# Last layer and output projection with the features in rows, in an attention block with a gated feed-forward network

## Chip, cores and metric

The kernel runs on one core of a Trainium2 chip. The metric is the device time of one execution in microseconds, the median of several runs; a profile of one further execution is shown beside it. The engines are named as the profile names them: PE (TensorE, matmuls; PEld are its weight loads), DVE (VectorE), ACT (ScalarE), POOL (GpSimd) and SP (the engine whose queue issues nearly all DMAs here).

## What is computed

The input is x of 8 sequences, each of 512 tokens with 256 features. Cut to what matters:

```python
xn = layernorm(x)                                   # over the 256 features
q, k, v = heads(xn @ in_proj_w.T)                   # 16 heads of 16; q and k are then rotated
p = softmax(where(0 <= t - s < 250, q @ k.T / 4, -inf))
s_ = merge(p @ v) @ out_proj_w.T                    # attention, 256 features
h = 2 * relu(s0 * concat(xn, -xn) @ sign(k0))       # 1024 features
h = 2 * relu(s1 * h @ sign(k1))                     # 1024
z = s2 * h @ sign(k2)                               # 256: the last layer
out = x + s_ * silu(z)
```

sign(k) is 1 where the boolean k holds and -1 elsewhere.

## The kernel before

Everything is written out without loops on the chip, one sequence b after another; B = 8, T = 512, P = 128. Within a sequence x is normalized with the tokens in the partitions (norm), turned on PE so that the features lie in the partitions (turn_x), and projected to v, k and q (project_v, project). The rotated q and k go to DRAM and come back in groups of four heads (to_dram, stack; on SP). Attention runs in nine steps: scores (sc, in two PSUM tiles), exponentials on ACT, masks on POOL (affine_select), and one step later the product with v (po). po has one PSUM bank; after a group of heads, keep (L690) empties it to V and S, on ACT for even groups and on DVE for odd ones. S holds the sums of the softmax; divisions inverts it in four pieces (L754), and divide shuffles it to R and multiplies V by R on POOL (L763), with a comparison on POOL (L767) and a count on DVE (L772) behind.

The feed-forward layers are exact in two parts: each activation is held as an f16 high part and an fp32r low part, so that h1, h2 and z take one set of matmuls for each (layer, L415; last, L441). Of a finished block of h, ACT writes the high part (L426) and then DVE the low part (L424); after the second the PSUM bank is free. ps_m has three such banks, tag "mm", shared by turn_x, v, q, k, h1, h2, z and the projection.

last makes z for 128 tokens at a time: the tokens are the stationary side, so z has the tokens in its partitions and 256 features in its columns. DVE scales it to gate (L467). gate_ready makes silu from it: an exponential on ACT (L496), the addition of 1 on POOL (L499), a reciprocal on DVE (L503) and a product on POOL (L504). project_o does the output projection for the same 128 tokens (att_ps, L782), fetches the same rows of x once more (xr, L787), multiplies by the gate on DVE (L804), adds xr on POOL (L809) and stores (L810). In the last sequence h2 is made in two halves of 256 tokens; z 0 and 1 are "soon", z 2 and 3 "final": their exponential comes straight from PSUM (L450), the reciprocal is L459, and the last output takes its own way (L794 to L798).

The order on each engine is the program's order, and a planner writes it. Each piece has a key, in units of which a sequence has SEQ = 42, and a cost; run sorts the pieces by key and sends follow-ups (pairs of a delay and a function) when the clock of summed costs has passed them. The layers of sequence b+1 begin at SEQ * (b + 1), and the z of sequence b stand between its h1 blocks:

```python
return SEQ * (b + 1) + 2 * L1 * (t + 1) + L3 * t            # last_at, b + 1 < B
return SEQ * (b + 1) + (32.0 + 3.2 * t if b + 2 < B else 18.0 + 2.5 * t)   # late
```

last_at is the key of z, late that of the projection, and gate_ready comes 4 units ahead of it. The pieces of attention are then placed among the keys of the layers (quick).

Of the kernel before, what the change touches and what calls it, by code (L numbers as in the profile page):

```python
# [11 lines left out]
F32 = mybir.dt.float32  # L12
# [4 lines left out]
ALU = mybir.AluOpType  # L17
# [17 lines left out]
def tile_attention_times_gated_ffn(  # L35
    ctx: ExitStack,
    tc: tile.TileContext,
    x: bass.AP,
    w_qkv: bass.AP,
    w_o: bass.AP,  # L40
    k0: bass.AP,
# [1 line left out]
    k2: bass.AP,  # L43
    s: bass.AP,
    rope: bass.AP,
    out: bass.AP,
):

# [22 lines left out]
    nc = tc.nc  # L73
    P = 128
    B, T, E = x.shape
    H = HEADS
    D = E // H
    NT = T // P
    EC = E // P
    F0, F1 = k0.shape[1], k1.shape[1]  # L80
    NF0, NF1 = F0 // P, F1 // P
# [10 lines left out]
    turned = ctx.enter_context(tc.tile_pool(name="turned", bufs=1))  # L92
    work = ctx.enter_context(tc.tile_pool(name="work", bufs=2))
# [105 lines left out]
    SEQ = 42.0  # L199
    L1, L2, L3 = 0.87, 3.45, 1.87  # L200
    states = {}
# [224 lines left out]
        high = lambda: nc.scalar.activation(hi, ph, AF.Relu)  # L426
        return [(0.0, high), (0.6 if f + 1 < NF0 else 0.0, low)]

    def last(b, t, how):
        st = states[b]  # L430
        pz = ps_m.tile([P, E], F32, tag="mm", name=f"z_ps_{b}_{t}")
        if how == "at once":
            for c in range(NF1):
                nc.tensor.matmul(
                    pz, st["h2p"][:, c, ts(t, P)], w2["l"][:, c].bitcast(F32),
                    start=(c == 0), stop=(c == NF1 - 1),
                )
        else:
            for p in "hl":
                for c in range(NF1):  # L440
                    nc.tensor.matmul(  # L441
                        pz, st["h2" + p][:, c, ts(t, P)], w2[p][:, c],
                        start=(c == 0 and p == "h"), stop=(c == NF1 - 1 and p == "l"),
                    )
        gate = st["gate", t] = outs.tile([P, E], F32, tag=f"gate{t}", name=f"gate_{b}_{t}")
        if how == "final":
            den = denominator(b, t)

            def ends():
                nc.scalar.activation(den, pz, AF.Exp, scale=scales[:, 1:2])  # L450
                nc.vector.tensor_scalar(gate, pz, scales[:, 0:1], None, ALU.mult)
                return [(0.3, add)]

            def add():
                nc.scalar.activation(den, den, AF.Identity, bias=1.0)
                return [(0.3, invert_)]

            def invert_():
                nc.vector.reciprocal(den, den)  # L459
                if t + 1 < NT:  # L460
                    nc.gpsimd.tensor_tensor(gate, gate, den, ALU.mult)
                st["den"] = den

            return [(0.0, ends)]

        def scale():
            nc.vector.tensor_scalar(gate, pz, scales[:, 0:1], None, ALU.mult)  # L467
            if how != "later":
                return [(0.5 if t == 0 else 4.5, lambda: gate_ready(b, t))]

        return [(0.0, scale)]

# [14 lines left out]
                    )  # L487
                nc.scalar.activation(h[:, f], ps, AF.Relu)

    def denominator(b, t):  # L490
        return work.tile([P, E], F32, tag="den", name=f"den_{b}_{t}")

    def gate_ready(b, t):
        st = states[b]
        gate, den = st["gate", t], denominator(b, t)
        nc.scalar.activation(den, gate, AF.Exp, scale=-1.0)  # L496

        def add():
            nc.gpsimd.tensor_scalar(den, den, 1.0, None, ALU.add)  # L499
            return [(0.9, invert_)]  # L500

        def invert_():
            nc.vector.reciprocal(den, den)  # L503
            return [(1.8, lambda: nc.gpsimd.tensor_tensor(gate, gate, den, ALU.mult))]  # L504

        return [(0.5, add)]

# [1 line left out]

    HALF = NF1 * L2 / 2 + 2 * L3  # L510

    def last_at(b, t):

        if b + 1 < B:
            return SEQ * (b + 1) + 2 * L1 * (t + 1) + L3 * t
        half = t // 2
        return SEQ * b + NF0 * L1 + NT * L3 + HALF * (half + 1) - 2 * L3 + L3 * (t % 2)

    def late(b, t):

        if b + 1 == B and t >= NT // 2:
            return last_at(b, NT - 1) + L3 + 0.9 * (t - NT // 2)
        if b + 1 == B:
            return SEQ * b + 40.0 + 0.9 * t
        return SEQ * (b + 1) + (32.0 + 3.2 * t if b + 2 < B else 18.0 + 2.5 * t)

    def finish_ffn(b, t, how):
        quick.add(last_at(b, t))
        out = [(last_at(b, t), L3, lambda: last(b, t, how))]
        if how == "later":  # L530
            out.append((late(b, t) - 4.0, 0, lambda: gate_ready(b, t)))
        return out

    def ffn(b):

        now = SEQ * b + (NT * L3 if b == 0 else 0)
        out = []
        for f in range(NF0):
            quick.add(now)
            out.append((now, L1, lambda f=f: layer(b, "h1", "x", w0, f)))  # L540
            now += L1
            if f % 2 and b > 0:
                now += L3
        if b + 1 == B:
            for half in range(2):
                cols = ts(half, T // 2)
                for f in range(NF1):
                    quick.add(now)
                    out.append((
                        now, L2 / 2,  # L550
                        lambda f=f, cols=cols: layer(b, "h2", "h1", w1, f, cols=cols),
                    ))
                    now += L2 / 2
                now += 2 * L3
            return out
        for f in range(NF1):
            quick.add(now)
            for i in range(2):
                out.append(
                    (now, L2 / 2, lambda f=f, i=i: layer(b, "h2", "h1", w1, f, i, 2))  # L560
                )
                now += L2 / 2
        return out
# [211 lines left out]

        return [(2.0, product)]

    def project_o(b, t, final=False):
        st = states[b]
        pp = ps_m.tile([P, E], F32, tag="mm", name=f"att_ps_{b}_{t}")  # L780
        for c in range(EC):
            nc.tensor.matmul(  # L782
                pp, st["V", c][:, ts(t, P)], wo_sb[:, c, :],
                start=(c == 0), stop=(c == EC - 1),
            )
        xr = work.tile([P, E], F32, tag="xr", name=f"xr_{b}_{t}")
        nc.sync.dma_start(xr, x[b, ts(t, P), :])  # L787
        st["xr", t] = xr
        if final and t + 1 == NT:
            att = work.tile([P, E], F32, tag="xn", name=f"att_{b}_{t}")  # L790

            def out_of_psum():
                y, den = st["gate", t], st["den"]
                nc.scalar.copy(att, pp)  # L794
                nc.gpsimd.tensor_tensor(y, y, att, ALU.mult)
                nc.vector.tensor_tensor(y, y, den, ALU.mult)
                nc.vector.tensor_tensor(y, y, xr, ALU.add)
                nc.sync.dma_start(out[b, ts(t, P), :], y)  # L798

            return [(0.0, out_of_psum)]  # L800

        def product():
            y = st["gate", t]
            nc.vector.tensor_tensor(y, pp, y, ALU.mult)  # L804
            return [(1.0 if final else 0.5, store)]

        def store():
            y = st.pop(("gate", t))
            nc.gpsimd.tensor_tensor(y, y, xr, ALU.add)  # L809
            nc.sync.dma_start(out[b, ts(t, P), :], y)  # L810

        return [(0.0, product)]

    def finish(b, final=False):
        out = []
        for t in range(NT):
            end = final and t >= NT // 2
            out.append((late(b, t), 0.87, lambda t=t, end=end: project_o(b, t, end)))
        return out

    def divisions(b):
# [42 lines left out]
        everything.append((at, 0, lambda f=f, w=w, e=engine: make_w1(f, w, e)))  # L864
    for b in range(B):
        everything += prepare(b) + ffn(b)
        for t in range(NT):
            how = "later" if b + 1 < B else "soon" if t < NT // 2 else "final"
            everything += finish_ffn(b, t, how)
            if b + 1 < B:  # L870
                at = SEQ * b + 1.5 if b else 2.0
                everything.append((at + t, 0, lambda b=b, t=t: load_x(b + 1, t)))
        everything += divisions(b) + finish(b, b + 1 == B)
# [55 lines left out]
    with tc.If(found < n_rows):  # L929
        for b in range(B):  # L930
            for t in range(NT):
                load_x(b, t)
            run(prepare(b, plain=True))
            plain_ffn(b)
            for t in range(NT):
                run(finish_ffn(b, t, "at once"))
            for g in range(NG):
                stack(b, g)
                po = ps_o.tile([P, T], F32, tag="po", name=f"f_po_{b}_{g}")
                for t in range(NT):  # L940
                    for r in range(4):
                        shifted(b, g, t, r, po)
                keep(b, g, po)
            run(divisions(b))
            run(finish(b))
# [58 lines left out]
```

## Time and profile before

| | us |
|---|---|
| median of 3 runs | 627.94 (627.25 to 629.54) |
| the profiled execution, its own time | 628.36 |
| its span in the profile | 626.6 |
| from one kb_ps to the next, sequences 1 to 6 | 75.0 |

| engine | busy us | idle us before its work, largest cause |
|---|---|---|
| PE | 608.6 | 2.8, the identity matrix at the start |
| DVE | 394.1 | 48.5, h2l for ACT's h2h |
| ACT | 299.7 | 140.2, h2h for PE's h_ps |
| POOL | 316.2 | 104.0, masks for ACT's p |

Busy time counts an instruction from its start to its end. Matmuls overlap in the profile, so that what one costs is read from the distance between starts. A line of a group gives the line of the kernel, the engine, the operation, the tile written and the tile read, partitions by elements, and how many there were. The granted clock was 0.996 of full speed over the span.

### The profile page before, as it was taken

The numbers are of one execution on the slowest core, as the hardware profiler recorded it, in microseconds if no ns is written. First come the engines' busy times: TensorE is split into PE (matmuls) and PEld (weight loads), VectorE is DVE, ScalarE is ACT, GpSimd is POOL, SyncE is SP. The second block draws the span as 40 slices with busy tenths as digits, with TensorE's granted clock in tenths as the row PEclk, the third lists the DMA queues.
The fourth block names the chain that finished last, engine by engine and source line by source line (L and its number), as shares of the span: only waits on it lengthen the run. The fifth ranks groups of instructions, "written<-read, shape, count | busy, mean of one in ns | idle before, by whom it ended". The sixth has DMA issues, their size and how long they took to land.

```text
span 626.6 us, 12051 instructions
## 1 busy us (share of the span) xinstructions
PE 608.6 (97%) x4842; PEld 398.4 (64%) x4842; DVE 394.1 (63%) x667; ACT 299.7 (48%) x441; POOL 316.2 (50%) x409
## 2 busy tenths in 40 slices
PE   8899999999999999999999999999999999999994
PEld 6455576556665567655676566765676556767793
DVE  6773535667575774766658576485665668456573
ACT  4566655534554445545354454453444544564411
POOL 2954542456533655427634366235662356638641
PEclk9999999999999999999999999999999999999998
DMA  9352721116311263114421252412532116230101
GB/s 273 117 197 95 260 85 51 51 68 216 122 51 51 87 208 110 52 51 172 139 93 51 75 214 76 143 33 86 208 94 88 51 69 227 77 109 19 53 18 48
DMA packets 38193, 67.20 MB, mean 107 GB/s; under 512 B 5104, under 2 KB 19184, under 8 KB 38128
## 3 DMA queue, kind: packets, MB, share of 16 engines
q1 hardware_dynamic: 36384, 64.24, 30.5%
q10 hardware_dynamic: 1744, 2.10, 1.0%
q8 instruction: 40, 0.66, 0.4%
q14 instruction: 25, 0.20, 0.1%
HBM read 36.96 MB, written 29.36 MB: 106 GB/s over the span
## 4 chain that ended last, share of the span: by engine, by line
PE 85%; DVE 5%; POOL 3%; DMA 3%; ACT 2%; issue 1%; SPq 0%; POOLq 0%; ACTq 0%; DVEq 0%
PE h_ps L415 41%; PE po L679 11%; PE z_ps L441 9%; PE sc L605 8%; PE v_ps L292 4%; PE att_ps L782 4%; PE qa_ps L307 2%; PE kb_ps L307 2%; PE qb_ps L307 2%; DMA kb<-in_k_dram 2%; PE ka_ps L307 2%; PE xnT_ps L268 1%; DVE den L503 1%; DVE h2l L424 1%; DVE xn L250 1%
## 5 line engine op out<-in xcount | busy, mean ns | idle before, releaser
L624 ACT ACTIVATE p<-sc 128x1024 f32<-128x1024 f32 (+2 forms) x144 | 138.5, 1013 | 75.0 <-PE sc L605 41.0
L415 PE MATMUL h_ps<-h1l,w1l_sb 128*128 128x512 f32 (+1 forms) x576 | 144.2, 392 | 0.0
L640 POOL TENSOR_SCALAR_AFFINE_SELECT p<-p 128x512 f32<-128x512 f32 x128 | 90.3, 711 | 104.0 <-ACT p L624 104.0
L415 PE MATMUL h_ps<-h1h,w1h_sb 128*128 128x512 f16 (+1 forms) x576 | 123.0, 356 | 0.5 <-ACT v_pad L299 0.5
L415 PEld LDWEIGHTS h_ps<-h1l,w1l_sb 128*128 128x128 f32 x576 | 99.5, 188 | 25.7 <-issue 6.8
L426 ACT ACTIVATE h2h<-h_ps 128x512 f16<-128x512 f32 (+1 forms) x72 | 39.6, 550 | 140.3 <-PE h_ps L415 140.2
L415 PEld LDWEIGHTS <-w1h_sb 128*128 128x128 f16 x576 | 51.5, 98 | 55.1 <-issue 13.4
L679 PE MATMUL po<-p,v_pad 128*32 128x378 f32 (+4 forms) x1216 | 77.2, 372 | 1.3 <-DVE S L703 1.1
L647 POOL TENSOR_SCALAR_AFFINE_SELECT p<-p 128x512 f32<-128x512 f32 (+1 forms) x96 | 50.0, 521 | 54.6 <-ACT p L624 49.7
L424 DVE SCALAR_TENSOR_TENSOR h2l<-h_ps,h2h 128x512 fp32r<-128x512 f32 (+1 forms) x72 | 44.3, 617 | 48.5 <-ACT h2h L426 48.5
L503 DVE RECIPROCAL den<-den 128x256 f32<-128x256 f32 x30 | 52.5, 1752 | 28.2 <-POOL den L499 28.1
L424 DVE SCALAR_TENSOR_TENSOR h1l<-h_ps,h1h 128x512 fp32r<-128x512 f32 x64 | 42.4, 675 | 34.8 <-ACT h1h L426 34.8
L605 PEld LDWEIGHTS sc<-q,k 32*128 32x128 f32 x1216 | 44.1, 184 | 26.1 <-issue 15.0
L754 DVE RECIPROCAL S<-S 128x128 f32<-128x128 f32 x64 | 58.9, 933 | 0.0
L426 ACT ACTIVATE h1h<-h_ps 128x512 f16<-128x512 f32 x64 | 38.2, 597 | 41.8 <-PE h_ps L415 41.2
L605 PE MATMUL sc<-q,k 32*128 32x378 f32 (+4 forms) x1216 | 57.2, 306 | 0.0
L415 PE MATMUL h_ps<-xl,w0l_sb 128*128 128x512 f32 x128 | 52.5, 491 | 0.0
L679 PEld LDWEIGHTS po<-p,v_pad 128*32 128x32 f32 x1216 | 31.3, 109 | 30.8 <-issue 16.2
L809 POOL TENSOR_TENSOR gate<-gate,xr 128x256 f32<-128x256 f32 x31 | 25.1, 810 | 46.8 <-DMA xr<-in_x_dram 41.2
L441 PE MATMUL z_ps<-w2l_sb,h2l 128*128 128x256 f32 x256 | 38.3, 291 | 0.4 <-DVE h2l L424 0.4
L415 PE MATMUL h_ps<-xh,w0h_sb 128*128 128x512 f16 x128 | 38.6, 383 | 0.0
L339 POOL TENSOR_TENSOR m_ka<-m_ka,m_kb 128x512 f32<-128x512 f32 x16 | 20.1, 1278 | 30.3 <-DVE m_kb L319 30.3
(97 smaller groups left out, 811.0 us busy)
## 6 DMA issues: line engine op xcount, KB each, us to landing
q<-dq SPq DMA_DIRECT2D x64, 256.0 KB, 3.6
dq<-qh SPq DMA_DIRECT2D x16, 512.0 KB, 3.4
dq<-m_qa SPq DMA_DIRECT2D x16, 512.0 KB, 5.0
k<-dk SPq DMA_DIRECT2D x32, 256.0 KB, 2.8
dk<-kh SPq DMA_DIRECT2D x8, 512.0 KB, 2.6
dk<-m_ka SPq DMA_DIRECT2D x8, 512.0 KB, 2.6
xr<-in_x_dram SPq DMA_DIRECT2D x32, 128.0 KB, 2.8
out_dram<-gate SPq DMA_DIRECT2D x32, 128.0 KB, 1.7
```

What stands on the lines that cost most here:

```text
L307: nc.tensor.matmul(ps, wqkv_sb[:, c, ds(col, P)], st["xT"][:, c, :], start=(c == 0), stop=(c == EC - 1),)
L415: nc.tensor.matmul(ph, w[p][:, c, ts(f, P)], st[src + p][:, c, cols], start=(k == 0), stop=(k == n - 1),)
L424: nc.vector.scalar_tensor_tensor(lo, ph, 0.0, hi, ALU.max, ALU.subtract)
L426: high = lambda: nc.scalar.activation(hi, ph, AF.Relu)
L441: nc.tensor.matmul(pz, st["h2" + p][:, c, ts(t, P)], w2[p][:, c], start=(c == 0 and p == "h"), stop=(c == NF1 - 1 and p == "l"),)
L503: nc.vector.reciprocal(den, den)
L605: nc.tensor.matmul(sc[r // 2][:, r % 2, ds(off, n)], st["k0", g][row, ts(j, P)], st[f"q{turn}", g][row, ds(j * P + first, n)], start=(turn ...
L624: nc.scalar.activation(p[:, 2 * half : 2 * half + 2, :n], sc[half][:, :, :n], AF.Exp, scale=D ** -0.5,)
L640: nc.gpsimd.affine_select(out=block, in_=block, compare_op=ALU.is_ge, fill=0.0, base=0, pattern=[[0, 4], [1, P]], channel_multiplier=-1,)
L647: nc.gpsimd.affine_select(out=block, in_=block, compare_op=ALU.is_ge, fill=0.0, base=-1, pattern=[[0, 4], [-1, beyond]], channel_multiplier=1,
L679: nc.tensor.matmul(po[32 * r : 32 * r + 32, ds(j * P + first, n)], v_columns(j, g, r), p_[:, r, ds(off, n)], start=(j == 0), stop=(done an ...
L754: nc.vector.reciprocal(part, part)
```

## The change

last and project_o swap their operands: the weights are the stationary side, so that z, gate, the projection and the result have 128 features in the partitions and the tokens in the columns. For sequences 0 to 6 there are two outputs u of 512 tokens in place of four of 128 tokens; for the last there are four of 256 tokens, u = 0 and 1 being the first half of the tokens. The kernel takes x a second time, transposed by the host (x_t), for the sum, and returns the result transposed. xr is fetched by residual, which is now called where the gate is made and no longer after the projection. xr and den have one buffer of 512 columns in place of two of 256; in the last sequence two outputs share one (beside), and xr of its second half stands in a tile that k and q no longer need. The reciprocal of a gate is done in two halves. In sequences 0 to 6 four h1 blocks now come before each z, where two did. In the last sequence all four projections come after the last z; the first two came in the second half of h2. Delays and keys are set anew.

```diff
+    def outputs(b):
+        n = 1 if b + 1 < B else 2
+        return [(f, ts(half, T // n)) for half in range(n) for f in range(EC)]
+
+    def beside(b, u, tag):
+        st = states[b]
+        if b + 1 == B and u % 2:
+            return st[tag][:, T // 2 :]
+        if b + 1 == B and u == 2 and tag == "xr":
+            st[tag] = turned.tile([P, 2, T], F32, tag="mb", name=f"xr_{b}_{u}", bufs=1)[:, 0]
+        else:
+            st[tag] = work.tile([P, T], F32, tag=tag, name=f"{tag}_{b}_{u}", bufs=1)
+        return st[tag][:, : T // 2] if b + 1 == B else st[tag]
+
+    def residual(b, u):
+        f, cols = outputs(b)[u]
+        xr = states[b]["xr", u] = beside(b, u, "xr")
+        nc.sync.dma_start(xr, x_t[b, ts(f, P), cols])
...
-        pz = ps_m.tile([P, E], F32, tag="mm", name=f"z_ps_{b}_{t}")
+        pz = ps_m.tile([P, T], F32, tag="mm", name=f"z_ps_{b}_{u}")
+        if b + 1 == B:
+            pz = pz[:, : T // 2]
...
-                        pz, st["h2" + p][:, c, ts(t, P)], w2[p][:, c],
+                        pz, w2[p][:, c, ts(f, P)], st["h2" + p][:, c, cols],
...
         if how == "final":
-            den = denominator(b, t)
+            residual(b, u)
+            den = beside(b, u, "den")
...
-                return [(0.5 if t == 0 else 4.5, lambda: gate_ready(b, t))]
+                return [(7.5 if u == 0 else 11.0, lambda: gate_ready(b, u))]
...
-    def gate_ready(b, t):
+    def gate_ready(b, u):
+        residual(b, u)
+        gate, den = st["gate", u], beside(b, u, "den")
         nc.scalar.activation(den, gate, AF.Exp, scale=-1.0)
+        width = T // 2 if b + 1 == B else T
 
         def add():
             nc.gpsimd.tensor_scalar(den, den, 1.0, None, ALU.add)
-            return [(0.9, invert_)]
-
-        def invert_():
-            nc.vector.reciprocal(den, den)
-            return [(1.8, lambda: nc.gpsimd.tensor_tensor(gate, gate, den, ALU.mult))]
+            return [(0.9 + 1.1 * k, lambda k=k: invert_(k)) for k in range(2)]
+
+        def invert_(k):
+            part = den[:, ts(k, width // 2)]
+            nc.vector.reciprocal(part, part)
+            if k == 1:
+                return [(1.8, lambda: nc.gpsimd.tensor_tensor(gate, gate, den, ALU.mult))]
...
-            return SEQ * (b + 1) + 2 * L1 * (t + 1) + L3 * t
+            return SEQ * (b + 1) + 4 * L1 * (u + 1) + 2 * L3 * u
...
-        if b + 1 == B and t >= NT // 2:
-            return last_at(b, NT - 1) + L3 + 0.9 * (t - NT // 2)
         if b + 1 == B:
-            return SEQ * b + 40.0 + 0.9 * t
-        return SEQ * (b + 1) + (32.0 + 3.2 * t if b + 2 < B else 18.0 + 2.5 * t)
+            return last_at(b, 3) + L3 + 0.9 * u
+        return SEQ * (b + 1) + (33.5 + 6.4 * u if b + 2 < B else 19.2 + 5.0 * u)
...
-            out.append((late(b, t) - 4.0, 0, lambda: gate_ready(b, t)))
+            out.append((late(b, u) - 4.5, 0, lambda: gate_ready(b, u)))
...
-            if f % 2 and b > 0:
-                now += L3
+            if f % 4 == 3 and b > 0:
+                now += 2 * L3
...
+        pp = ps_m.tile([P, T], F32, tag="mm", name=f"att_ps_{b}_{u}")
+        if b + 1 == B:
+            pp = pp[:, : T // 2]
         for c in range(EC):
             nc.tensor.matmul(
-                pp, st["V", c][:, ts(t, P)], wo_sb[:, c, :],
+                pp, wo_sb[:, c, ts(f, P)], st["V", c][:, cols],
...
-        xr = work.tile([P, E], F32, tag="xr", name=f"xr_{b}_{t}")
-        nc.sync.dma_start(xr, x[b, ts(t, P), :])
...
-            nc.sync.dma_start(out[b, ts(t, P), :], y)
+            nc.sync.dma_start(out_t[b, ts(f, P), cols], y)
...
-        for t in range(NT):
-            end = final and t >= NT // 2
-            out.append((late(b, t), 0.87, lambda t=t, end=end: project_o(b, t, end)))
+        for u in range(len(outputs(b))):
+            end = final and u >= 2
+            out.append((
+                late(b, u), 1.75 if b + 1 < B else 0.87,
+                lambda u=u, end=end: project_o(b, u, end),
+            ))
```

## The prediction

> **What bounds the kernel now.** I read the busy table first, then TensorE's own waits, then its timeline, since only the timeline gives what a step costs.
>
> ```profile
> PE 608.6 (97%) x4842; PEld 398.4 (64%) x4842; DVE 394.1 (63%) x667; ACT 299.7 (48%) x441; POOL 316.2 (50%) x409
> ```
>
> ```profile
> PE po L679 <- DVE S L703: 1.1, 1, 1.1
> PE z_ps L441 <- DVE h2l L424: 0.4, 1, 0.4
> PE po L679 <- POOL p L647: 0.2, 1, 0.2
> ```
>
> TensorE (PE) is full, and its list of waits holds 8 us in all, 2.8 of them for the identity at the start. The largest totals of the general list, ACT waiting 140.2 for h_ps and POOL 41.2 for xr, are other engines waiting for PE or for something that PE doesn't need. So only two things move the time: what PE's stream costs, and what PE waits for.
>
> ```profile
> 323.81 1.05 PE L441 MATMUL z_ps<-w2h_sb,h2h 128*128 128x256 f16 x8
> 324.61 1.19 PE L441 MATMUL z_ps<-w2l_sb,h2l 128*128 128x256 f32 x8
> 325.64 0.60 PE L415 MATMUL h_ps<-xh,w0h_sb 128*128 128x512 f16 x2
> ...
> 335.98 1.90 PE L415 MATMUL h_ps<-h1h,w1h_sb 128*128 128x512 f16 x8
> 337.53 2.20 PE L415 MATMUL h_ps<-h1l,w1l_sb 128*128 128x512 f32 x8
> 339.57 0.38 PE L268 MATMUL xnT_ps<-ident,xn 128*128 128x128 f32 x2
> ```
>
> Columns: start, length, instruction. Read the starts, not the lengths: sixteen matmuls of 256 columns take 325.64 - 323.81 = 1.83 us, sixteen of 512 take 339.57 - 335.98 = 3.59.
>
> **What the skill says.** "Perfetto Trace Analysis", Identifying the Most-Contended Engine, calls matmul busy time a bad measure because matmuls are pipelined; the trace agrees (mean length of a 256-column z matmul 274 to 291 ns, step 114). "TensorE: Matmul & The Clock Gate", Back-to-back issue gap, gives 262 cycles for 256 columns and 518 for 512, so that a matmul's fixed part is tiny; the trace agrees in kind: 114 and 224 ns. "Perfetto Trace Analysis", Optimizing Scalar/DVE Operations, says that each instruction has a fixed access cost; here ACT's f16 copy from PSUM takes 478 ns for 256 elements and 597 for 512. "PSUM — Partial Sum Buffer", The four PSUM rules, has a bank hold 512 fp32 of one matmul's output: the new z tile fills a bank, the old one half; no row shows what that costs.
>
> **The change, part by part.** I number sequences 0 to 7 and the outputs of one u.
>
> *Last layer, sequences 0 to 6.* Four z blocks of 1.83 us become two of sixteen 512-column matmuls. The same mix of f16 and f32 costs 3.59 in the h2 block above: 4 x 1.83 - 2 x 3.59 = 0.14 us saved (0.16 with a third digit). The 16 weight loads that go in each pair, 98 or 188 ns, lie under matmuls already: the step of 114 is below 188.
>
> *Projection, sequences 0 to 6.* At 374.42 an h2 block with a projection inside takes 378.88 - 374.42 = 4.46; less 3.59, a projection costs 0.87. A 512-column one is like qa_ps: four records from 357.14 to 358.86, 1.72. Four times 0.87 against two of 1.72 saves 0.04. So PE saves 0.18 to 0.20 us a sequence, 1.3 in seven.
>
> *Elementwise work.* Per sequence DVE's 4 scales (0.48) and 4 products (0.41) become 2 and 2 of about 0.70 and 0.68 (V from PSUM 0.74, rope product 0.68): 3.6 to 2.8. The reciprocals stay 4 of 1.75. ACT's 4 exponentials of 0.41 become 2 of about 0.62 (between 0.60 and 0.70 for its 512-wide rows). POOL's 4 of 0.85 + 0.76 + 0.81 become 2 of 1.50 + 1.29 + 1.29 (rows R and V): 9.7 to 8.2. All this lies beside PE's work, so I take 0; the cover is that no engine but PE is over 63%. If the cover fails, it is by order: see the first rival.
>
> *xr and the result.* SP issues 4 DMAs a sequence in place of 8, each of 256 KB (q<-dq of that size lands in 3.6 us, the old xr in 2.8), xr now with the gate, 4.5 key units (some 8 us, at 75.0 us for 42 units) ahead of the projection, where it came right after it. POOL's 41.2 us of waiting should go; it frees POOL, not PE. With one xr buffer, the xr of u=1 waits on SP for POOL's sum of u=0; behind it stand the store of u=1 and, by the keys, the q and k loads of group 1, due 6.6 units later. Between 0 and, if those loads came late by half a POOL sum, 0.65 us a sequence; I take 0. One den buffer in place of two: u=1 starts 6.4 units, some 11 us, after u=0, whose chain takes 0.62 + 1.50 + 2 x 1.75 + 1.29 = 6.9: 0.
>
> *Last sequence, middle.* Two stalls of PE are there now:
>
> ```profile
> 570.98 0.90 PE L605 MATMUL sc<-q,k 32*128 32x244 f32 x24
> 572.99 1.50 PE L679 MATMUL po<-p,v_pad 128*32 128x378 f32 x24 [1.11 <-DVE S L703]
> ```
>
> ```profile
> 590.54 1.08 PE L441 MATMUL z_ps<-w2l_sb,h2l 128*128 128x256 f32 x7
> 592.03 0.39 PE L441 MATMUL z_ps<-w2l_sb,h2l 128*128 128x256 f32 x1 [0.41 <-DVE h2l L424]
> ```
>
> In the first, po needs its bank, DVE empties it (keep, L703) only after den's reciprocal of 569.87. In the new order both reciprocals of the first gate of sequence 6 stand before keep. scores come 1.83 later there (a z block more precedes), so POOL's masks, V times R and the addition (1.5) end near 568.9; reciprocal to 570.65, h2l, reciprocal to 572.8, keep to 574.3. PE asks at 570.02 + 1.72 + 0.83 = 572.6: 1.7 of stall for 1.17, so +0.5 (0 to +1). The second is h2l behind the count that waits for POOL; the new order puts the count behind h2l: -0.77 (the block took 2.61 for 1.83; -0.77 to 0).
>
> *The end.* Projections 0 and 1 of the last sequence, 1.73 us of PE, move from the second half of h2 to behind z 3. PE's total is unchanged, but what follows z changes:
>
> ```profile
> 615.57 1.89 PE L782 MATMUL att_ps<-wo_sb,V 128*128 128x256 f32 x8
> ...
> 616.92 1.74 DVE L459 RECIPROCAL den<-den 128x256 f32<-128x256 f32 x1
> ...
> 618.58 0.36 DVE L804 TENSOR_TENSOR gate<-att_ps,gate 128x256 f32<-128x256 f32 x1
> ...
> 619.02 0.83 POOL L809 TENSOR_TENSOR gate<-gate,xr 128x256 f32<-128x256 f32 x1 [0.34 <-DVE gate L804]
> ...
> 620.61 1.14 SPq L810 DMA_DIRECT2D out_dram<-gate  x1
> ```
>
> Count from the start of z 2 (611.90). Now the last store is issued at 8.7. New: reciprocal of z 3 until 6.95 (5.02 + 1.74, plus queueing), then three DVE products of 0.40; the fourth projection needs a third bank and gets it at 7.35, after the first product; it ends at 8.5, its copy at 8.9. POOL's sums of 0 and 1 end at 8.8 by then, so its product runs 8.9 to 9.7, DVE's last two operations to 10.9, and the last store goes at 11.3. Less the 1.73 by which z 2 starts earlier: 9.6 for 8.7, +0.9 (-0.5 if the products slip ahead, +1.7 if the whole move shows).
>
> **Sum.** -1.3 + 0.5 - 0.77 + 0.9 = -0.7. The profiled execution took 628.36 us (span 626.6 and 1.76 around it), 0.42 above the median of 627.94; it would be 627.7, and the median 627.2. Less than 0.5%, 3.1 us, is about what a measurement of this kernel can tell from no change.
>
> **Rivals.**
> *Slower: the third h1 block finds no bank.* At the head of a sequence PE now issues h1, v, h1, v, then z at 316.65; the new order has an h1 block there and z three steps later. It takes the bank that the first h1's low part frees, at 316.02 today: 0.63 of slack.
>
> ```profile
> 315.34 0.68 DVE L424 SCALAR_TENSOR_TENSOR h1l<-h_ps,h1h 128x512 fp32r<-128x512 f32 x1
> ...
> 316.65 1.04 PE L441 MATMUL z_ps<-w2h_sb,h2h 128*128 128x256 f16 x8
> ```
>
> Ahead of it on DVE stand the product of u=1, the last h2l, which comes 1 us later since the projection now stands inside its block, keep (2 x 0.75) and the count; I get 316.5, a slack of 0.15. From 0.15 more each delay goes to PE seven times: at 0.8, 7 x 0.65 = 4.6, and 631.8. For it: v_ps waited for h1l twice (1.6). Against: POOL's wait for xr goes. Chance 0.15.
> *Faster: both stalls of the last sequence go and the end is hidden.* 1.3 + 1.17 + 0.77, and a quarter of the 4.6 us that weight loads of po wait for POOL: -4.4, 623.6. Against: DVE has the same reciprocals. Chance 0.20.
> *Faster: weight loads count.* If half the 8 x 188 ns of f32 loads of each pair showed, 14 x 0.75 = 10.5, 617.4; the step of 114 speaks against. Chance 0.07, most of it for smaller gains.
> *It doesn't do what it says:* xr blocks SP and q or k come late, 7 x 0.65 = 4.6 more, 631.8. Chance 0.05.
> The main case keeps 0.53, with 625 to 630 of its own: its unknown costs are -0.77 to +1, -0.5 to +1.7.
>
> **Numbers.** Predicted 627.2. Range 623.0 to 632.0: both neighbours are in, the weight-load case out. Faster 0.07 + 0.20 = 0.27, same 0.53, slower 0.15 + 0.05 = 0.20.
>
> **What would show it.** A z block of 512 steps 3.59 and a projection 1.72; the period of sequences 1 to 6 (75.0 from kb_ps to kb_ps) shrinks by 0.2; POOL's wait for xr is gone; PE waits for DVE S once, near 1.7 long, not for h2l; the last store goes 0.9 later after z 2, moved up by 1.73. A shorter step, or a period 0.5 off, would prove me wrong; a bank wait of PE or of its weight loads on h1l in each sequence speaks for the first rival.

## The result, and the profile after

| | before | after |
|---|---|---|
| median of 20 runs, us | 628.87 (627.25 to 630.34) | 627.05 (625.61 to 627.90) |
| the profiled execution, its own time | 628.36 | 627.78 |
| its span | 626.6 | 626.0 |

The ratio is 0.9972, with a 95% interval of 0.9964 to 0.9981: 1.8 us less, inside the 0.5% that the prediction called no change. That the time came so near 627.2 is luck: the median of before moved from 627.94 in three runs to 628.87 in twenty, 0.9 us up, and the gain was 1.8 us where the prediction saw 0.7, 1.1 more. The two errors cancel.

The busy table and PE's list of waits of the kernel after, beside those shown of before:

```profile
PE 606.8 (97%) x4562; PEld 374.1 (60%) x4562; DVE 382.2 (61%) x641; ACT 299.2 (48%) x427; POOL 309.4 (49%) x367
```

```profile
PE po L708 <- DVE S L732: 1.2, 1, 1.2
...
PE att_ps L815 <- DVE gate L835: 0.7, 1, 0.7
```

DVE and POOL are busy for 12 and 7 us less, and PE is as full as before. Of DVE's 12 us, 7 are not work that went away: the same 32 xn took 23.4 us before and 16.1 after (the last section says why an xn varies). The wait of z for h2l is gone from the list; a wait of the last projection for a bank is new. In POOL's list the 41.2 us for xr ahead of L809 (L840 now) are gone too. It shows 11.1 us ahead of gate L536 under the name of xr, but L536 does not read xr: the list has 6.5 us more of the same wait as "issue", and in experiment 5, where xr was fetched elsewhere, all of it, 17.5, stands as "issue". A releaser is inferred.

The timeline of PE, one z of 512 columns:

```profile
320.90 1.90 PE L469 MATMUL z_ps<-h2h,w2h_sb 128*128 128x512 f16 x8
322.45 2.22 PE L469 MATMUL z_ps<-h2l,w2l_sb 128*128 128x512 f32 x8
324.51 1.02 PE L295 MATMUL v_ps<-wqkv_sb,xT 128*128 128x256 f32 x4
```

The starts give 324.51 - 320.90 = 3.61 us; the prediction took 3.59. The timeline of DVE and PE at the first stall of the last sequence:

```profile
567.68 1.75 DVE L534 RECIPROCAL den<-den 128x256 f32<-128x256 f32 x1 [2.89 <-POOL den L529]
569.62 1.74 DVE L534 RECIPROCAL den<-den 128x256 f32<-128x256 f32 x1
571.85 0.74 DVE L732 SCALAR_TENSOR_TENSOR S<-po,s_sb,S 128x512 f32<-128x512 f32 x1
572.74 1.50 PE L708 MATMUL po<-p,v_pad 128*32 128x378 f32 x24 [1.23 <-DVE S L732]
```

Both reciprocals now stand ahead of keep, as forecast, and the stall is 1.23 us for 1.11. The timeline at the end:

```profile
611.82 2.75 PE L815 MATMUL att_ps<-V,wo_sb 128*128 128x256 f32 x12
613.24 1.74 DVE L490 RECIPROCAL den<-den 128x256 f32<-128x256 f32 x1
614.90 1.02 DVE L835 TENSOR_TENSOR gate<-att_ps,gate 128x256 f32<-128x256 f32 x3
615.31 1.13 PE L815 MATMUL att_ps<-V,wo_sb 128*128 128x256 f32 x4 [0.74 <-DVE gate L835]
619.53 0.38 SPq L841 DMA_DIRECT2D out_dram<-gate  x1
```

The fourth projection waits until the first DVE product has emptied a bank, and the last store goes 11.37 us after the start of z 2 (608.16), where it went at 8.71.

I sorted PE's starts by kind of block, to see where the profiled 0.6 us came from. Up to the kb_ps of sequence 1: +1.02, but this start-up varies from profile to profile (the kernels below with the same start have their first kb_ps anywhere between 13.2 and 14.4). From there to the kb_ps of sequence 7, six sequences: -2.04. From there to z 2: -2.72, of which 1.73 is the moved projections. From z 2 to the last store's issue: +2.66. From there to the end of the span: 5.95 before, 6.51 after, +0.56. Without the start-up that makes -1.54, near the 1.8 of the medians.

### The profile page after: what moved, and what is told of

Same layout as the page of the kernel before. It is cut to its first block, busy times and chain, and to the rows that moved or that the text cites. A ratio compares the mean times of both kernels' runs of the same rounds, so it can differ in the third digit from the quotient of the medians.

```text
span 626.0 us, 11319 instructions
## 1 busy us (share of the span) xinstructions
PE 606.8 (97%) x4562; PEld 374.1 (60%) x4562; DVE 382.2 (61%) x641; ACT 299.2 (48%) x427; POOL 309.4 (49%) x367
## 5 line engine op out<-in xcount | busy, mean ns | idle before, releaser
L669 POOL TENSOR_SCALAR_AFFINE_SELECT p<-p 128x512 f32<-128x512 f32 x128 | 93.4, 736 | 133.6 <-ACT p L653 133.5
L534 DVE RECIPROCAL den<-den 128x256 f32<-128x256 f32 (+1 forms) x32 | 52.6, 1645 | 25.2 <-POOL den L529 25.2
L783 DVE RECIPROCAL S<-S 128x128 f32<-128x128 f32 x64 | 57.4, 919 | 0.0
L469 PE MATMUL z_ps<-h2l,w2l_sb 128*128 128x512 f32 (+1 forms) x144 | 35.8, 390 | 0.0
L295 PE MATMUL v_ps<-wqkv_sb,xT 128*128 128x256 f32 x128 | 33.1, 381 | 2.6 <-DVE h1l L427 1.6
L342 POOL TENSOR_TENSOR m_ka<-m_ka,m_kb 128x512 f32<-128x512 f32 x16 | 20.1, 1273 | 30.3 <-DVE m_kb L322 30.3
```

What stands on the lines that cost most here:

```text
L295: nc.tensor.matmul(v.rearrange("p n s d -> p (n s d)"), st["xT"][:, c, ts(t, P)], wqkv_sb[:, c, 2 * E :], start=(c == 0), stop=(c == EC - 1),)
L469: nc.tensor.matmul(pz, w2[p][:, c, ts(f, P)], st["h2" + p][:, c, cols], start=(c == 0 and p == "h"), stop=(c == NF1 - 1 and p == "l"),)
L534: nc.vector.reciprocal(part, part)
L669: nc.gpsimd.affine_select(out=block, in_=block, compare_op=ALU.is_ge, fill=0.0, base=0, pattern=[[0, 4], [1, P]], channel_multiplier=-1,)
L783: nc.vector.reciprocal(part, part)
```

## The experiments

Each was timed against the kernel before, which had a median of 628.9 to 629.0 in all three groups of runs. By *period* I mean the distance of two kb_ps in sequences 2 to 7: 74.9 to 75.2 before, 74.6 to 74.7 after, 74.98 and 74.63 in the mean. (From sequence 1 to 2 it is longer in every kernel, 75.70 before and 75.40 after.)

**1. What is the width worth?** The new kernel, each 512-column z and projection issued as two halves:

```diff
-                    nc.tensor.matmul(
-                        pz, w2[p][:, c, ts(f, P)], st["h2" + p][:, c, cols],
+            for part in (ts(0, T // 2), ts(1, T // 2)) if b + 1 < B else (cols,):
...
+                        nc.tensor.matmul(
+                            pz[:, part] if b + 1 < B else pz,
+                            w2[p][:, c, ts(f, P)], st["h2" + p][:, c, part],
```

(project_o likewise.) 

> The changed kernel, but in sequences 0 to 6 each 512-column matmul of z and of the projection is cut into two of 256 columns in the same bank; everything else, orders and layout, stays. Theory A (the gain of the layout is PE's step per matmul, 0.18 to 0.20 us a sequence): the period from kb_ps to kb_ps rises from 74.63 to 74.81 to 74.84, z steps 3.66 for 3.59 to 3.61, and the whole is 1.3 us slower than the changed kernel (627.05), 628.3. Rival B (the order and the waits bring the gain, the matmuls' width nothing): period 74.63, 627.0. Rival C (every weight load costs): period over 75.5, over 633.

Measured: 627.88, ratio 0.9983 [0.9976, 0.9990], period 74.75. The width is worth 0.12 us a sequence (0.09 in z, 0.02 in the projection and the h2 around it), seven times that is 0.8, and the median moved by 0.8. The prediction's term had the right cause and was over half too large, 1.3 for 0.8; and less than half of the measured gain is due to it.

**2. The order of the blocks alone.** The kernel before with four h1 blocks ahead of each pair of 256-column z:

```diff
-            return SEQ * (b + 1) + 2 * L1 * (t + 1) + L3 * t
+            return SEQ * (b + 1) + 4 * L1 * (t // 2 + 1) + L3 * t
...
-            if f % 2 and b > 0:
-                now += L3
+            if f % 4 == 3 and b > 0:
+                now += 2 * L3
```

> The kernel before with one part of the change: the h1 blocks come in fours, with two z blocks of 256 columns together after each four (last_at and ffn), so that v and the attention steps fall between as in the changed kernel; layout, outputs of 128 tokens, xr and the end as before. Theory A (besides the layout's 0.2, the period fell by another 0.15 to 0.2 because of the order: v no longer stands ahead of scores, 0.13, and po waits less for masks, 0.07): period 74.75 to 74.85 for 75.0, and the whole 1.0 to 1.4 us faster than before. Rival B (all of the period's gain is the layout's): period 75.0, no change. Rival C (fours of h1 run out of PSUM banks): slower, period over 75.3, PE or its weight loads waiting for h1l.

Measured: 626.44, ratio 0.9953 [0.9939, 0.9967], period 74.51 to 74.57 but for one of 74.95. This one step of the change, which I had costed at nothing, gains at least as much as the whole: 2.5 us for 1.8, though the two intervals overlap at their edges. The one long period, 74.95, is a single po block of 1.34 us in place of 0.98; the next section has its cause. Part of the gain the whole change has as well: over five sequences v takes 17.25 us for 17.88 and h1 37.26 for 37.00, together 0.07 less in each. Another part it has not: the h2 blocks and transposes around the second half of norm take 0.38 less. The timeline of the kernel after suggested why, at V times R:

```profile
339.30 1.27 POOL L792 TENSOR_TENSOR V<-V,R 128x512 f32<-128x512 f32 x1
339.98 0.73 DVE L253 TENSOR_SCALAR xn<-x,mv,rstd 128x256 f32<-128x256 f32 x1
341.37 0.20 PEld L271 LDWEIGHTS xnT_ps<-ident,xn 128*128 128x128 f32 x2 [0.53 <-DVE h2l L427]
```

The third xn of the sequence (L253) runs beside POOL's product and takes 0.73 us; the two that run alone at 336.02 take 0.40 each. It stands ahead of h2l on DVE, and h2l holds the bank that the next transpose needs. In the kernel with the order alone POOL's product comes earlier, this xn takes 0.40, and the transpose waits 0.20. Experiment 7 tests that reading. With the order alone the timeline of POOL and DVE also shows that it isn't enough for the two to overlap:

```profile
338.68 1.50 POOL L767 TENSOR_SCALAR R<-S 128x512 f32<-128x512 f32 x1
339.24 0.40 DVE L250 TENSOR_SCALAR xn<-x,mv,rstd 128x256 f32<-128x256 f32 x1
```

This xn lies wholly within POOL's comparison and loses nothing; the last section comes back to it.

**3. The projections of the last sequence moved back to where they were**, on the new kernel, with the old delays of their gates:

```diff
-            return last_at(b, 3) + L3 + 0.9 * u
+            if u >= 2:
+                return last_at(b, 3) + L3 + 0.9 * (u - 2)
+            return SEQ * b + 40.0 + 0.9 * u
```

(gate_ready after 0.5 and 4.5 in place of 7.5 and 11.0.) 

> The changed kernel with its end undone: projections 0 and 1 of the last sequence return to the second half of h2 (keys 40.0 and 40.9), with the delays of their gates as before (0.5 and 4.5). Theory A (the move cost 0.9 us): from the start of z 2 to the last store 8.7 us for 11.4, z 2 1.73 later, and the whole 0.9 us faster than the changed kernel, 626.1. Rival B (the earlier gates bring DVE's reciprocals back ahead of h2l, and a stall before z 0 or z 1 of the last sequence eats it): the stall of some 0.8 is back, 627.0. Rival C (the end is hidden): no change and 11.4 stays for 9.6 plus 1.7, no.

Measured: 627.08, ratio 0.9965 [0.9952, 0.9979]: no difference. The end is short again (8.70), but one h2 block of the last sequence takes 3.48 us for 1.83. PE's timeline:

```profile
600.06 1.03 PE L418 MATMUL h_ps<-h1h,w1h_sb 128*128 128x256 f16 x8 [1.50 <-DVE h2l L427]
```

With the projections in the middle, their gates' reciprocals stand on DVE among those of S, all ahead of this h2l. So the move back gains nothing in the sum: what it wins at the end is lost here.

**4. The same move on the kernel before, by itself.**

```diff
-        if b + 1 == B and t >= NT // 2:
-            return last_at(b, NT - 1) + L3 + 0.9 * (t - NT // 2)
         if b + 1 == B:
-            return SEQ * b + 40.0 + 0.9 * t
+            return last_at(b, NT - 1) + L3 + 0.9 * t
```

> The kernel before, with nothing changed but projections 0 and 1 of the last sequence moved behind its z 3. It measures the prediction's last term by itself. Theory A, as in the prediction: z 2 starts 1.73 earlier, the last store goes 11.3 instead of 8.7 us after it, +0.9, the whole 629.8 for 628.9. Theory B: the projection blocks hid waits of h2 for h2l too, and without them z 2 starts less than 1.73 earlier: +1.5 to +1.8. Theory C: the moved work is hidden, 628.9.

Measured: 631.36, ratio 1.0036 [1.0023, 1.0049]: +2.4, above every expectation. The timeline of DVE at its end:

```profile
625.04 0.42 DVE L795 TENSOR_TENSOR gate<-gate,xr 128x256 f32<-128x256 f32 x1 [2.82 <-DMA xr<-in_x_dram]
```

The old project_o fetches xr with the projection, into two buffers. With four projections in a row the fetches of the last two wait for POOL's sums, and the last is issued at 622.86: the last store goes 13.60 us after z 2. The change fetches all four ahead, with their gates, and pays 11.37. The gates' delays were left as they were, and the z 0 block took 3.21 us in place of 2.61, so the relief there, which the changed kernel and experiment 3 have (1.92 and 1.91), did not come.

**5. xr fetched with the projection**, in sequences 0 to 6 of the new kernel:

```diff
     def gate_ready(b, u):
-        residual(b, u)
+        if b + 1 == B:
+            residual(b, u)
...
     def project_o(b, u, final=False):
+        if b + 1 < B:
+            residual(b, u)
```

> The changed kernel, but in sequences 0 to 6 xr is fetched with the projection, as before the change, and not with the gate. Theory A (POOL's wait for xr is hidden): POOL waits again, 14 times, for xr some 2 to 3 us each (30 to 40 us in all), the period stays 74.63 within 0.05, the whole 627.05 within 0.5. Rival B (POOL's wait holds masks up, so that po waits): the period rises by 0.1 to 0.3, mostly in po, 0.7 to 2 us in all; weight loads of po wait for POOL again, over 4 us in all.

Measured: 630.98, ratio 1.0036 [1.0023, 1.0049], 3.9 us more than the kernel after, periods 74.66 to 75.73. The timeline of SP's queue, POOL and PE:

```profile
374.65 1.61 SPq L374 DMA_DIRECT2D q<-dq  x2
376.31 0.42 SPq L452 DMA_DIRECT2D xr<-in_x_t_dram  x1
379.56 1.28 POOL L843 TENSOR_TENSOR gate<-gate,xr 128x512 f32<-128x512 f32 x1 [2.36 <-DMA xr<-in_x_t_dram]
389.17 1.13 PE L295 MATMUL v_ps<-wqkv_sb,xT 128*128 128x256 f32 x4 [0.17 <-DVE gate L838]
```

xr is issued at 376.31, behind the loads of k and q for group 0, where the kernel after issues it at 370.17, ahead of them. POOL waits 2.36 us, does the addition, V times R and the gate's product of u=1 that much later, and DVE's product of u=1 (which empties a bank) is late at the head of the next sequence. There the first blocks take 1.25 (h1), 0.97 (v) and, two blocks on, 1.51 (v), for 0.91, 0.86 and 0.86.

**6. The same, but xr of u=0 fetched ahead of those loads:**

```diff
+            ahead = 1.6 if b + 2 < B else 0.0
+            out.append((late(b, u) - 0.001 - (ahead if u == 0 else 0.0), 0, lambda: residual(b, u)))
```

> The new kernel with xr fetched as in the run before (ahead of its projection, not with the gate), but the fetch of u=0 now stands 1.6 key units earlier, ahead of stack's loads of q and k for group 0 on SP. Theory A, the order on SP made the 3.9 us: xr comes in time again, the period of sequences 1 to 6 is 74.65 (74.63 with the gate, 74.93 to 75.73 behind the loads), the whole 627.1, and POOL's wait for xr stays under 0.5 us for each u=0. Theory B, xr has to be fetched some 8 us ahead, the order on SP doesn't matter: 629.5 to 631, with h1 and v longer at the head of each sequence.

Measured: 627.37, ratio 0.9973 [0.9962, 0.9984], period 74.64 to 74.67. The loss is gone. xr is now issued at 369.74: the 1.6 key units, some 2.9 us, moved it by 6.6, and the rest is what SP had stood in the loads. So the cost of experiment 5 is the time that its place in SP's queue gave this one fetch, and u=1, fetched with its projection, does no harm.

**7. V times R taken away from xn.** The new kernel, the divide of pair 1 at key 10.4 in place of 12.2:

```diff
+                last_ = first + 4 * d if pair == 0 else SEQ * (b + 1) + 10.4
...
-            out.append((first + d * 4, 0, lambda p=pair: divide(b, p)))
+            out.append((last_, 0, lambda p=pair: divide(b, p)))
```

> The new kernel with the divide of pair 1 (shuffle on DVE, V times R on POOL) at key 10.4 in place of 12.2, ahead of the scale of z 1. Theory A, the gain of the order alone came from xn not running beside V times R: the third xn takes 0.40 us for 0.73, the second transpose waits 0.2 for 0.53 us, the period goes from 74.63 to 74.3 (74.2 to 74.4), the whole from 627.05 to 624.8 (624 to 625.5). Theory B, the wait of the transpose has another cause (h2l's place on DVE): xn gets shorter, the wait stays at 0.5, 627.0. Theory C, the shuffle ahead of the scale keeps z's bank 0.7 us longer and the third h1 block waits for it: 627.5 to 630.

Measured: 625.00, ratio 0.9940 [0.9928, 0.9952], period 74.33 to 74.37. The timeline, to be held against that of experiment 2:

```profile
333.77 1.27 POOL L792 TENSOR_TENSOR V<-V,R 128x512 f32<-128x512 f32 x1 [1.92 <-DVE R L789]
338.73 0.45 DVE L253 TENSOR_SCALAR xn<-x,mv,rstd 128x256 f32<-128x256 f32 x1
339.83 0.22 PEld L271 LDWEIGHTS xnT_ps<-ident,xn 128*128 128x128 f32 x2 [0.25 <-DVE h2l L427]
```

The third xn takes 0.45 and the transpose waits 0.25 for 0.53. The first two xn now run beside POOL's product and comparison and take 0.97 and 0.77 for 0.40, and nothing waits for them: the sum of all xn rose from 16.1 to 20.1 us while the kernel became faster. The period lost 0.29, h2 and transposes 0.28. The stall of po for keep in the last sequence fell from 1.2 to 0.7 as well, which I had not foreseen.

**8. That, and the end short without the stall of experiment 3:** projections 0 and 1 of the last sequence at keys 42.0 and 44.0, their gates after 5.0 and 6.0. 

> The run before it, with projections 0 and 1 of the last sequence back in the second half of its h2 at keys 42.0 and 44.0, later than in the kernel before (40.0 and 40.9), and their gates made ready after 5.0 and 6.0 in place of 7.5 and 11.0, so that the reciprocals do not stand in one row ahead of h2l. Theory A: the end is short (8.7 us from the start of z 2 to the last store, 11.37 less 1.73 with all four projections there), and the h2 block's wait for h2l (1.50 with keys 40.0 and 40.9) is under 0.6: 0.3 to 0.9 us less than the run before, 624.2. Theory B, the reciprocals stand ahead of h2l wherever they are put in that half: the wait is over 1.2, and it is 625.0, no better than the run before.

Measured: 624.17, ratio 0.9919 [0.9906, 0.9932]. The gain is as expected, the working only in part: the h2 block's wait for h2l is 0.9 us, not under 0.6. The last store is issued 8.70 us after z 2.

**9. And the count of pair 1 later in the last sequence,** because that h2l stood behind it:

```diff
-            return [(4.0 if b + 1 < B else 1.5, count)]
+            return [(4.0 if b + 1 < B or pair == 1 else 1.5, count)]
```

> The version with the early shuffle and the short end, and the count of pair 1 in the last sequence 2.5 later, behind two more h2l. It had left one wait of PE for h2l (0.9 us, the block from 601.84 takes 1.90 for 0.86 + its share), where h2l stands on DVE behind a count that waits 0.78 us for POOL. Theory A: nothing else of PE's stands behind that POOL work (the last masks are over by then), so the wait goes and the whole is 0.9 less, 623.3. Theory B: as with count_alone, the wait comes back at the next thing behind it, 624.2.

Measured: 623.53, ratio 0.9914 [0.9901, 0.9927]. From the kb_ps of sequence 7 to z 2 it takes 1.04 us less, the block of 1.90 now 0.86; the median moved by 0.6. This is the best version, 3.5 us below the changed kernel.

**10 and 11. The stall at z 0 in the kernel before.** First the same edit for pair 0 there:

```diff
-            return [(4.0 if b + 1 < B else 1.5, count)]
+            return [(4.0 if b + 1 < B or pair == 0 else 1.5, count)]
```

> The kernel before with one change: the count of pair 0 in the last sequence comes 2.5 later, behind the last h2l of sequence 7's first half. Theory A, as in the prediction: h2l stood behind a count that waited for POOL, so the z block takes 1.83 in place of 2.61 us, PE's wait for h2l (0.41, and what the weight loads take with it) is gone, and the whole is 0.77 less, 628.1 for 628.9. Theory B, the wait is bought back a few us later on the same chain: the z block is 1.83 and the rest of the last sequence 0.4 to 0.8 longer, 628.7.

Measured: 628.89, ratio 0.9999 [0.9991, 1.0007]. No gain. The h2l is early and the z block has no wait within it, but PE's timeline shows the wait one block later:

```profile
593.16 1.41 PE L679 MATMUL po<-p,v_pad 128*32 128x244 f32 x16 [0.76 <-POOL p L647]
```

The two blocks are no shorter (2.76 and 1.34 for 2.61 and 1.17): the masks of this p stand on POOL behind the same V times R and comparison that the count had waited for. So the second edit, on the kernel before, puts V times R and the comparison behind the masks: the product 3.0 after the shuffle in place of 2.0. 

> The kernel before with V times R of pair 0 in the last sequence started 1.0 later, so that POOL does the three masks of the last scores first and the count falls behind h2l as in count_alone, which gained nothing: its z block was short of the h2l wait, but po waited 0.76 us for a mask behind V times R. Theory A, POOL's order decided and h2l was only the first to show it: z block 1.83 to 1.92, po 0.98 to 1.17 with no wait, the whole 0.8 less, 628.1 for 628.9. Theory B: a third waiter takes it over (keep, or the reciprocals behind the count), 628.8.

Measured: 628.97, ratio 1.0003 [0.9995, 1.0012]. z 0 takes 1.93 and its po 0.98, without a wait, and still nothing is gained:

```profile
600.73 1.03 PE L415 MATMUL h_ps<-h1h,w1h_sb 128*128 128x256 f16 x8 [0.58 <-DVE gate L467]
...
603.49 0.71 PE L415 MATMUL h_ps<-h1h,w1h_sb 128*128 128x256 f16 x5 [0.79 <-DVE h2l L424]
```

The count now holds up DVE until 596.04, behind it stand the gate's scale, keep, the reciprocal of den and three of S, and only then h2l. Two h2 blocks take 2.56 and 2.76 for 1.83: 1.66 lost, for 0.87 won at z and po. The profile says +0.8, the medians 0; either way the stall moved.

## Why the prediction was right, and where it was not

*Last layer and projection, -1.3.* Right in cause, mis-sized: 0.12 a sequence and 0.8 in all by experiment 1, for 0.18 to 0.20 and 1.3. The z step of 3.59 came from an h2 block; a z takes 3.61, and the two of a sequence 7.31 for 7.41. The skill's page "TensorE: Matmul & The Clock Gate", Back-to-back issue gap, which the prediction used for the kind alone, gives a better size: two of 262 cycles for one of 518 save 6; with the trace's 224 ns for 518 cycles, 40 such pairs in a sequence make an estimate of 0.10. Steps read to 0.01 us from blocks in other places don't resolve that.

*Elementwise work and order of blocks, 0.* This is the step that failed. The period shrank by 0.35, not 0.2. Beside the width's 0.12 there are 0.10 for v and h1 in their new order (experiment 2 shows 0.07 of it) and 0.07 for po. What remains, 0.06, is within the h2 blocks and isn't assigned.

The part of po is one block of 16 in each sequence, which waits for the mask of L647. The timeline of POOL and PE in the kernel before:

```profile
159.17 0.74 POOL L809 TENSOR_TENSOR gate<-gate,xr 128x256 f32<-128x256 f32 x1 [2.10 <-DMA xr<-in_x_dram]
159.86 1.28 POOL L763 TENSOR_TENSOR V<-V,R 128x512 f32<-128x512 f32 x1
161.10 0.64 POOL L647 TENSOR_SCALAR_AFFINE_SELECT p<-p 128x512 f32<-128x512 f32 x1
...
162.00 1.20 PE L679 MATMUL po<-p,v_pad 128*32 128x244 f32 x16
```

The masks stand on POOL behind the sum that waits for xr and behind V times R. Over five sequences the block took 0.98 where that sum waited 1.2 to 1.3 us and 1.08 to 1.13 where it waited 1.5 to 2.1; the 1.34 of experiment 2 had a wait of 2.56. In the changed kernel the masks stand ahead of V times R and end 2.8 us before the block, which takes 0.98 in all five; in experiment 5 as well, where POOL waits for xr again. So it is POOL's order, not its lighter load, that took the wait away; which of the new keys and delays made that order was not isolated. "It frees POOL, not PE" was wrong by this 0.07: a late xr did reach PE.

One reading of the prediction is of two different copies: the 478 ns for 256 elements are those of xh, which also scales, and the 597 for 512 those of h2h. The same h2h copy takes 385 ns for 256. No term rests on it.

*xr with the gate, 0.* The value was right, but only because of how the change places the fetch: with the projection as before and the new keys it costs 3.9 (experiment 5). The rival that xr blocks SP had its resource right and its direction reversed: it is xr that falls behind k and q.

*keep, +0.5.* The mechanism was right, the size not: +0.1. The new kernel is 1.2 us earlier here, so count from the start of the projection block ahead (570.02 in the forecast, 568.79 measured). POOL ended its addition 1.15 before it, where I had 1.1. But the second reciprocal ended 2.57 after it and not 2.8, keep's two operations took 1.23 us and not 1.5, so that the bank was free at 3.80 and not 4.3; and PE asked for it at 2.72, not 2.6.

*h2l behind the count, -0.77.* The block went from 2.61 to 1.92, -0.69. The reason given, the count's place behind h2l, is not enough: experiments 10 and 11 made that order and gained nothing, as masks, then the bank of the gate's scale and a later h2l took the wait over. In the changed kernel the same order costs nothing later, because the moved projections have taken their gates' reciprocals out of this stretch of DVE: between the count and the next h2l stand the gates' scales, keep and three of S alone. With the gates put back (experiment 3) z 0 still takes 1.91, but PE then waits 1.50 for that h2l. The prediction booked the moved projections as a loss at the end alone.

*The end, +0.9.* 11.37 less 1.73 is 9.64 for 8.71: +0.93, with the bank wait at the place forecast. But the span ends 0.56 later still after the last issue, which the sum did not look at. The last store takes 3.84 us from its issue to its landing, for 3.00 before; it takes 3.75 to 3.84 in all five kernels that have the new layout and four projections at the end, and 2.90 to 2.95 in the three that put two of them back (experiments 3, 8 and 9). Why it lands later is open. Together 0.6 was forecast for the last sequence and its end, and the profile shows -0.99 + 0.93 + 0.56 = +0.5.

*The rivals.* The third h1 block did not wait for its bank. The timeline of DVE and PE:

```profile
315.28 0.68 DVE L427 SCALAR_TENSOR_TENSOR h1l<-h_ps,h1h 128x512 fp32r<-128x512 f32 x1
...
316.47 0.59 PE L418 MATMUL h_ps<-xh,w0h_sb 128*128 128x512 f16 x2
```

The low part ends at 315.96, 0.51 ahead of the matmul that needs the bank; I had reckoned 0.15. Experiment 5 shows that it was the right place to fear: the same head of a sequence loses its slack as soon as POOL is 2.4 us late. Weight loads did not count: a z of 512 columns steps no shorter than the h2 block. And the rival with both stalls gone and the end hidden did not come: po still waits 1.23 us, and the end costs 0.93.

## What to carry to other kernels

Where PE is full, cost the new order of blocks on PE and on the elementwise engines, and not only the operations: here the order alone was worth at least as much as the whole change, and one shuffle set 1.8 key units earlier another 2 us. A wait names only the first that stands behind a late piece of work; before booking its removal as a gain, list all that is queued behind the same piece, on each engine, since each of them takes the wait over in turn. When a DMA moves, read which DMAs it stands behind in its queue before and after.

## What was not expected of the hardware

DVE's xn (fp32, 256 columns, SBUF to SBUF) takes 0.40 us alone. Where it starts while POOL is at its product V times R, it ends 0.15 us after the product does, in all 78 cases of these traces: started 0.2, 0.46 or 0.68 us into the product, it takes about 1.23, 0.97 or 0.73. Beside POOL's masks it is the same in 42 cases (0.45 to 0.73). A constant end and not a constant factor means that xn is held until POOL's instruction is over, and is not merely slowed; why it then needs only 0.15 of its 0.40 isn't shown. The skill's page "SBUF — State Buffer", Who interferes with whom, says that DVE in a two-port mode and POOL contend for a shared pair of ports, and that whichever comes second is fully blocked for the whole instruction. For the product and the masks the traces fit that, though no run shows that xn is in such a mode.

POOL's comparison is different, as far as its recorded span goes (spans on POOL are rough). The xn that start with it, within 0.04 us, take 0.75 to 0.79 and end 0.74 or 0.75 ahead of its end, in 42 cases, the second xn of experiment 7 among them (over at 335.89; the comparison runs from 335.13 to 336.63). And the third xn of experiment 2, which starts 0.56 us into it, takes 0.40 in all six sequences. So no hold lasts for the whole of that instruction. What an xn's delay costs depends on the place only: 0.28 us a sequence where h2l stands behind it, nothing where nobody waits.

The block ahead of scores steps about 0.09 longer than its like in three kinds of block (z 3.70 for 3.61, h1 0.99 for 0.90, z of 256 columns 1.92 for 1.83). Why was not tested.
